# Four waits of TensorE in a graph network: sums of the first geglu quarter, a low part of step 0, last thirds of the last chunk, and the time of a load

## The chip, the cores and the metric

The kernel runs on one core of one Trainium2 chip. The time is device microseconds of one execution, the median of three runs. The profile is of one execution, with a span of its own.

## The reference

A graph network on 1024 nodes with 512 features, 16384 edges, and four transformer layers between two graph convolutions, all in fp32. Cut to what matters:

```python
h = gcn(batchnorm(relu(layernorm(x))), src, dst, gcn_in_w, gcn_in_b)
for i in range(4):
    q = ln(h) @ Wq[i]; k = cond @ Wk[i]; v = cond @ Wv[i]      # 16 groups of 64 nodes, 256 cond rows each
    h = h + softmax(q k^T / 8) v @ Wo[i]                        # 8 heads of 64
    val, gate = split(ln(h) @ geglu_w[i] + geglu_b[i])          # 2 x 2048 columns
    h = h + (val * gelu(gate)) @ ffo_w[i] + ffo_b[i]
out = x + gcn(h, src, dst, gcn_out_w, gcn_out_b) + relu(layernorm(x))
```

## The kernel before

TensorE (PE) does nearly all the work. Most products are not run as fp32 matmuls: an operand is split into a high part of twelve bits (names with h: `ah`, `bh`, `gr`, `gha`), a low part (l) and a third (s, made of the two), and three quick matmuls give what one slow one would. ACT makes high parts, DVE low parts by a SCALAR_TENSOR_TENSOR of two operands in SBUF, and POOL or DVE the thirds. `left_parts` does so for the moving side.

A layer goes through these stages:

- **Attention**, in steps g = 0 to 6 and one more. A step makes the scores of 128 nodes (`sc`, L831), their softmax (`nmax` and `pr` on DVE, the exponential on ACT), and beside them keys and values of the next step (`k`, `v`; `split_cond` splits the condition rows `ct` into `ah_c`, `al_c` and `as_c`, two tiles of each for a step; `base_of` makes one block of the final sum's base in two steps of a layer: the Relu `again` on ACT and two adds on DVE).
- **The first geglu quarter**, class `Quad`, four pieces c = 0 to 3. It runs as plain fp32 by a scheme of seven products, of which sums of sums are formed on DVE: `u2 = b + s1`, `u3 = c + u2`, `g1 = d + u3`, `g0 = c + u2`, with b, c and d the banks `gb`, `gc`, `gd`. Products 5, 6 and 4 fill b, c and d; product 3 then adds into c, so PE waits for u3 to have read it, and product 2 adds into d, so PE waits for g1. Between the sums `fill()` puts the next piece of splitting the right operands for the other quarters (`gr`, `gl`, lines 1017, 1025 and 1037) on DVE's queue. POOL sums thirds there (L1039) and weight sums (L1081).
- **The other three quarters**, chunks (r, c) with split operands (L1109). `split_rest` makes thirds of the next chunk's weights on POOL (`gsb`, `gs`). In the last chunk of a layer, (R-1, KC-1), `output.split(0, nc.gpsimd)` splits the first gated tile of the output product: `ah_f` on ACT, `al_f` on DVE, `as_f` on POOL.
- **The output product**, 16 units of 24 matmuls (L1252). Unit n fetches the gated tile `fr` of unit n + 2, splits that of n + 1, and runs what a table `beside` names for n. In the last layer that table loads the edge counts (`ce`, eight tiles, issued by POOL) for the last convolution, takes `w_out`, and splits it.

The order of each engine's instructions is fixed when the program is built: a scheduler orders what is not pinned, `pin` and `in_order` keep the written order, `tc.issue_after(x)` puts instructions behind x in the order, and `waiting_for(x, engine)` adds a real wait on x. Tiles come from pools: `slots` has 35 buffers of 512 KB, taken in turn, so a new tile waits for the last reader of the buffer that it gets. PSUM has 8 banks.

Of the kernel before, what the change touches and what calls it, by code (L numbers as in the profile page):

```python
# [15 lines left out]
OP = mybir.AluOpType  # L16
# [5 lines left out]
TINY = 2.0 ** -12  # L22
# [4 lines left out]
def gnn_kernel(  # L27
# [26 lines left out]
    nc = tc.nc  # L54
# [10 lines left out]
    KC = D // P  # L65
# [4 lines left out]
    R = DFF // D  # L70
# [235 lines left out]
    def twelve_bits(t):  # L306
        return t.bitcast(F32R)
# [3 lines left out]

    def left_parts(x, name, t=None):

        parts = [slots_of(len(x), f"{n}_{name}") for n in ("ah", "al", "as")]
        for h, l, s, x in zip(*parts, x):
            nc.scalar.mul(twelve_bits(h), x, INWARD * TINY)  # L318
            nc.vector.scalar_tensor_tensor(twelve_bits(l), h, -1.0 / TINY, x, OP.mult, OP.add)  # L319
            if t:  # L320
                t.tensor_tensor(twelve_bits(s), h, l, OP.subtract)  # L321
                continue
            for k in range(2):
                nc.gpsimd.tensor_tensor(twelve_bits(s)[:, k, :], h[:, k, :], l[:, k, :],  # L324
                                        OP.subtract)
        return parts
# [16 lines left out]
                        twelve_bits(s)[:, k, :], hk, -TINY, lk, OP.mult, OP.add)  # L343
        return parts

    def split_cond(l, g):
        if g < NG:
            if l == 0:
                save_cond(g)
            conds[g] = left_parts(raw_x.pop((l, g)), f"c_{l}_{g}")  # L350

    conds = {}

# [592 lines left out]
    class Quad:  # L946
# [27 lines left out]
        def rest(self, fill):  # L974
            n, bias = self.n, gcols[:, self.cv:self.cv + 1]
            b, c, d = (bank(f"{x}_{n}") for x in ("gb", "gc", "gd"))
            u2, u3 = (acc_tile(f"g{x}_{n}") for x in ("u2", "u3"))
            g0, g1 = (t512(f"{x}_{n}") for x in ("g0", "g1"))
            f0, f1 = self.f.of(self.c)

            def add(to, x, y):
                self.last = pin(nc.vector.tensor_tensor(to, x, y, OP.add))

            self.product(5, b, True, pin)
            add(u2, b, self.s1)
            fill()
            self.product(6, c, True, pin)
            add(u3, c, u2)
            fill()
            self.product(4, d, True, pin)  # L990
            add(g1, d, u3)
            self.gate(g1, n)
            fill()
            self.product(3, c, False, pin)
            add(g0, c, u2)
            self.gate(g0, n)
            fill()
            self.product(2, d, False, pin)
            add(d, d, u2)
            pin(nc.vector.scalar_tensor_tensor(f0, self.a, bias, g0, OP.add, OP.mult))  # L1000
            pin(nc.vector.scalar_tensor_tensor(f1, d, bias, g1, OP.add, OP.mult))
            self.f.store(self.c)
            fill()
            fill()
# [196 lines left out]
    class Output:  # L1201
# [8 lines left out]
                self.raw[n] = slot(f"fr_{self.l}_{n}")  # L1210
                nc.sync.dma_start(self.raw[n], f_dram[s, 2 * u:2 * u + 2].rearrange("c p n -> p c n"))

        def split(self, n, t=nc.vector):
            if n in self.raw:
                self.f[n] = left_parts([self.raw.pop(n)], f"f_{self.l}_{n}", t)

        def fetch_w(self, u):
            if u < UNITS:
# [206 lines left out]
    for l in range(L):  # L1425
# [157 lines left out]
        for g in range(NG - 1):  # L1583
            if g == NG - 2:
                take_ln3()
                raw = load_geglu(l, 0)
                add_bias(nc.vector)
            if not g:
                probs = scores(l, g, qT, kTs.pop(g))
            if g == NG - 2:  # L1590
                with waiting_for(scores.last, mybir.EngineType.Pool):
                    left = geglu_weights(l, 0, *raw)
            wo_flow = out_parts(l, wo) if not g else iter(())
            wo = next(wo_flow, wo)
            if g in (1, 2):
                fetch_x(2 * l + g - 1)
            k = keys(l, g + 1, wk, 1 if l == 0 and g == 0 else 0)
            for i, u in enumerate(k):
                u.begin()
                if not i:  # L1600
                    for end in ends:
                        end()
                if i > 1:
                    k[i - 2].end()
                next(wo_flow, None)
            k[-2].end()
            for _ in wo_flow:
                pass
            v = values(l, g + 1, wv)
            with in_order(mybir.EngineType.DVE) if g == NG - 2 else nullcontext():  # L1610
                oT = mix(l, g, probs, vs.pop(g), (
                    k[-1].end, nothing, lambda: (v[0].begin(), g == NG - 2 and
                                                 add_bias(nc.vector, *range(4)))))
            if g < NG - 2:
                probs = scores(l, g + 1, qT, kTs.pop(g + 1))
                with tc.issue_after(scores.last.ins):
                    oT = oT()
            if g == NG - 2:
                oT = oT()
                ln3_norm(g - 2, g - 1, behind=mix.last)  # L1620
                add_bias(nc.gpsimd, g - 2, g - 1)
            if g in (1, 2):
                with tc.issue_after(scores.last.ins):
                    base_of(2 * l + g - 1)
            if l == 0:
                fetch_cond(g + 3)
            split_cond(l, g + 2)
            if l:
                load_cond(l, g + 3)
            v[1].begin()  # L1630
            v[0].end()
            v[2].begin()
            v[1].end()
            pieces = attn_out(l, g, oT, wo, pin) if g < NG - 2 else iter(())
            next(pieces, None)
            if g in (3, 5):
                moments_into(mv_kept[:, 2 * (g - 3):2 * (g - 1)], [h[g - 3], h[g - 2]],
                             f"ln3_{l}_{g - 3}")
            if g == NG - 2:
                for nb in range(4):  # L1640
                    ln3_turn(nb, each=pin)
            v[3].begin()
            next(pieces, None)
            v[2].end()
            next(pieces, None)
            ends = [v[3].end]
            if g == NG - 3:
                scale_kept()
            if g == NG - 2:
                for nb in range(4, 6):  # L1650
                    ln3_turn(nb, each=pin)
                for nb in (g - 2, g - 1):
                    ln3_sums(nc.gpsimd, nb)
            if l == 0 and g + 3 < NG:
                turn_cond(g + 3, each=pin)
# [30 lines left out]
        def fill(n=1):  # L1686
            for _ in range(n):
                next(parts, None)
# [64 lines left out]
                load()  # L1753
        sum_chunk(2)

        def split_rest(short):
            long = begin_split(0, False)
            next(long, None)
            with waiting_for(split_left.low, mybir.EngineType.Pool):
                for flow in short, long:  # L1760
                    for _ in flow:
                        pass
# [4 lines left out]
        for r in range(1, R):  # L1767
            f = Gated(l, r)
            for c in range(KC):
                n = (r - R + 2) * KC + c  # L1770
                if n == -1:
                    output.fetch_w(0)
                if (r, c) == (R - 1, KC - 2):
                    output.fetch(0)
                chunk = ready.pop(0)
                flow = chunk.steps(lambda: before and sum_chunk(1))
                chunk.f = f
                next(flow)
                if 0 < n < 5:
                    next(ahead)  # L1780
                for _ in islice(short, 2):
                    pass
                next(flow)
                if before:
                    split_rest(short)
                    load()
                for _ in parts:
                    pass
                if (r, c) == (R - 1, KC - 1):
                    with in_order(mybir.EngineType.Activation), in_order(mybir.EngineType.DVE), \  # L1790
                            in_order(mybir.EngineType.Pool):
                        output.split(0, nc.gpsimd)
                    output.fetch(1)
                for step in range(3):
                    if before:
                        next(before, None)
                    next(flow)
                    if step == 1 and not before:
                        split_rest(iter(()))
                        load()  # L1800
                before = flow
                short = begin_split(0, True)
                if n == 0:
                    next(ahead)
# [9 lines left out]
        if last:  # L1814
# [15 lines left out]
                nonlocal w_out  # L1830
                w_out = right_parts(w_out, "w_out")

            beside = {8: begin_last, 9: fetch_counts, 12: fetch_last, 15: split_last}
        else:
            half = range(4), range(4, 8)
            wk, wv = [[], [], []], [[], [], []]
# [121 lines left out]
```

## Time and profile before

| | |
|---|---|
| median of 3 runs | 2298.52 us (2296.37 to 2298.68) |
| the profiled execution | 2296.64 us |
| its span | 2294.9 us |
| granted clock of PE | 1.0 throughout |
| busy: PE, DVE, ACT, POOL | 2265.4, 1734.6, 1168.7, 747.1 us |

A row of a timeline is: start, length, engine, line, operation, output <- inputs, shape, how many alike, and in brackets the idle time ahead of it and who ended it. A row of the waits is: who waited <- for whom, then us in total, how many times, and the longest. Lines are those of the kernel before.

### The profile page before, as it was taken

How to read it: one execution, taken by the hardware profiler on the slowest of the kernel's cores; microseconds unless marked ns; L12 is line 12 of the kernel's file. 1: busy time of each engine (PE TensorE's matmuls, PEld its weight loads, DVE VectorE, ACT ScalarE, POOL GpSimd, SP SyncE). 2: the span in 40 equal slices, each digit the busy share in tenths (PEclk: the TensorE clock that was granted, in tenths of full speed). 3: DMA queues.
4: the chain of work that ended last, by engine and by line, in shares of the span. 5: the costliest groups of instructions: out<-in, count | busy, mean ns of one | idle time of the engine just before them, and what ended most of it. 6: DMA issues, size and time to landing. Idle time of an engine off the chain costs nothing. (4 is left out here: it accounts for less than half of the span.)

```text
span 2294.9 us, 34482 instructions
## 1 busy us (share of the span) xinstructions
PE 2265.4 (99%) x12496; PEld 1754.5 (76%) x12496; DVE 1734.6 (76%) x3172; ACT 1168.7 (51%) x2245; POOL 747.1 (33%) x647
## 2 busy tenths in 40 slices
PE   8999999999999999999999999999999999999999
PEld 5678887587887888488887888578788888668777
DVE  9886556999986555989987554989987554899965
ACT  7555445565355445465356444556437444556521
POOL 1121213486021224377021222368112112268301
PEclk9999999999999999999999999999999999999999
DMA  6042211234411101133521111133531111043551
GB/s 206 2 152 70 74 61 42 83 120 152 169 46 65 61 29 42 60 119 99 200 92 65 51 38 42 42 107 100 184 138 56 37 52 51 1 129 111 184 173 57
DMA packets 144113, 204.42 MB, mean 89 GB/s; under 512 B 11240, under 2 KB 68912, under 8 KB 143936
## 3 DMA queue, kind: packets, MB, share of 16 engines
q1 hardware_dynamic: 141840, 196.72, 26.0%
q0 software_dynamic: 1376, 4.30, 0.6%
q8 instruction: 103, 1.69, 0.3%
q10 hardware_dynamic: 720, 1.11, 0.1%
q14 instruction: 74, 0.61, 0.1%
HBM read 151.75 MB, written 50.34 MB: 88 GB/s over the span
## 5 line engine op out<-in xcount | busy, mean ns | idle before, releaser
L324 POOL TENSOR_TENSOR as_c<-ah_c,al_c 128x512 fp32r<-128x512 f32 x128 | 197.7, 1574 | 901.0 <-DVE al_c L319 679.9
L1123 ACT ACTIVATE g<-g 128x512 f32<-128x512 f32 x192 | 112.5, 586 | 152.8 <-PE g L1109 151.5
L381 ACT ACTIVATE k<-k 128x512 f32<-128x512 f32 x125 | 73.0, 585 | 193.0 <-PE k L370 193.0
L1252 PE MATMUL fx<-bs_wff,as_f 128*128 128x512 f32 x512 | 159.0, 390 | 0.6 <-DVE as_f L321 0.6
L1252 PE MATMUL fy<-bl_wff,al_f 128*128 128x512 f32 x512 | 158.8, 390 | 0.6 <-DVE al_f L319 0.5
L318 ACT ACTIVATE ah_f<-fr 128x1024 fp32r<-128x1024 f32 x64 | 67.9, 1061 | 177.3 <-PE fy L1252 98.8
L1252 PE MATMUL fy<-bh_wff,ah_f 128*128 128x512 f32 x512 | 157.8, 390 | 0.2 <-ACT ah_f L318 0.2
L386 DVE COPY kT<-k 128x512 f32<-128x512 f32 x54 | 37.2, 689 | 156.8 <-PE k L370 156.8
L370 PE MATMUL v<-bh_wv,ah_c 128*128 128x512 f32 x508 | 140.9, 399 | 0.0
L370 PE MATMUL v<-bs_wv,as_c 128*128 128x512 f32 x508 | 137.1, 393 | 2.6 <-ACT v L381 2.6
L1050 POOL TENSOR_TENSOR gsa<-gha,gla 128x512 fp32r<-128x512 f32 x96 | 124.1, 1315 | 40.2 <-DVE gla L1045 40.2
L370 PE MATMUL v<-bl_wv,al_c 128*128 128x512 f32 x508 | 136.6, 390 | 0.0
L843 ACT ACTIVATE pr<-sc,nmax 128x256 f32<-128x256 f32 x256 | 118.1, 474 | 35.0 <-DVE nmax L838 34.5
L370 PE MATMUL k<-ah_c,bh_wk 128*128 128x512 f32 x500 | 135.1, 392 | 0.0
L381 ACT ACTIVATE v<-v 128x512 f32<-128x512 f32 x127 | 75.0, 591 | 116.9 <-PE v L370 116.9
L370 PE MATMUL k<-as_c,bs_wk 128*128 128x512 f32 x500 | 132.1, 395 | 1.8 <-ACT k L381 1.8
L370 PE MATMUL k<-al_c,bl_wk 128*128 128x512 f32 x500 | 133.8, 389 | 0.0
L1109 PE MATMUL g<-gr,gha 128*128 128x512 f32 x384 | 120.0, 394 | 0.0
L1109 PE MATMUL g<-gr,gsa 128*128 128x512 f32 x384 | 119.9, 393 | 0.0
L1109 PE MATMUL g<-gl,gla 128*128 128x512 f32 x384 | 118.3, 389 | 0.0
L370 PEld LDWEIGHTS v<-bs_wv,as_c 128*128 128x128 f32 x508 | 93.2, 188 | 27.7 <-ACT v L381 5.7
L370 PEld LDWEIGHTS v<-bh_wv,ah_c 128*128 128x128 f32 x508 | 92.6, 188 | 27.9 <-issue 9.2
(321 smaller groups left out, 5814.3 us busy)
## 6 DMA issues: line engine op xcount, KB each, us to landing
f_dram<-fT SPq DMA_DIRECT2D x128, 256.0 KB, 2.1
fr<-f_dram SPq DMA_DIRECT2D x64, 512.0 KB, 4.1
ct<-cond_dram SPq DMA_DIRECT2D x48, 512.0 KB, 4.7
wff<-in_L_gnn_ffo_w_dram SPq DMA_DIRECT2D x32, 512.0 KB, 5.2
gxb<-in_L_gnn_geglu_w_dram SPq DMA_DIRECT2D x96, 128.0 KB, 2.5
gxa<-in_L_gnn_geglu_w_dram SPq DMA_DIRECT2D x96, 128.0 KB, 2.6
cond<-in_L_gnn_cond_dram SPq DMA_DIRECT2D x32, 256.0 KB, 4.2
cond_dram<-ct SPq DMA_DIRECT2D x16, 512.0 KB, 3.3
```

Of the source, the lines that this page charges most:

```text
L318: nc.scalar.mul(twelve_bits(h), x, INWARD * TINY)
L324: nc.gpsimd.tensor_tensor(twelve_bits(s)[:, k, :], h[:, k, :], l[:, k, :], OP.subtract)
L370: pin(nc.tensor.matmul(self.bank, twelve_bits(left[k // 2])[:, k % 2, self.c * P:(self.c + 1) * P], twelve_bits(right[k // 2])[:, k % 2, : ...
L381: nc.scalar.mul(self.bank, self.bank, 1.0 + TINY)
L386: nc.vector.tensor_copy(self.to(), self.bank)
L843: nc.scalar.activation(pr3[:, a, :], ps3[:, a, :], AF.Exp, bias=nmax[:, a:a + 1], accum_out=tot[:, a:a + 1])
L1050: split_left.last = pin(t.tensor_tensor(s_at, h_at, l_at, OP.subtract))
L1109: pin(nc.tensor.matmul(to, self.part(i, which)[:, k, :], self.rights[i][which].bitcast(F32R)[:, k, :], start=start and k == 0, stop=stop a ...
L1123: pin(nc.scalar.mul(to, to, 1.0 + TINY))
L1252: pin(nc.tensor.matmul(to, twelve_bits(left[which][0])[:, k, b * P:(b + 1) * P], twelve_bits(right[which])[:, k, :], start=u == 0 and whic ...
```

## The change

It has four parts.

- **A.** In `Quad.rest` the number of fills between the sums changes: in c=0 one more fill behind u2, in c=1 and c=2 u3 directly behind u2 and both fills behind u3.
- **B.** `split_cond` splits its two tiles one by one. In step 0 of each layer the second is put behind `scores.last`, the last instruction of the softmax. `base_of` now also waits for that instruction on ACT.
- **C.** In the last chunk `split_rest` is called from within `output.split`, between al_f and as_f, and its POOL instructions wait for al_f instead of for the low part of the chunk's weights.
- **D.** In the last layer the counts are loaded at unit 11 instead of 9.

```diff
@@ left_parts
-    def left_parts(x, name, t=None):
+    def left_parts(x, name, t=None, between=None):
...
-            nc.vector.scalar_tensor_tensor(twelve_bits(l), h, -1.0 / TINY, x, OP.mult, OP.add)
+            left_parts.low = nc.vector.scalar_tensor_tensor(twelve_bits(l), h, -1.0 / TINY, x,
+                                                            OP.mult, OP.add)
+            if between:
+                between()
@@ split_cond
-    def split_cond(l, g):
+    def split_cond(l, g, behind=None):
...
-            conds[g] = left_parts(raw_x.pop((l, g)), f"c_{l}_{g}")
+            conds[g] = [[], [], []]
+            for i, x in enumerate(raw_x.pop((l, g))):
+                with tc.issue_after(behind.ins) if behind and i else nullcontext():
+                    for to, of in zip(conds[g], left_parts([x], f"c_{l}_{g}_{i}")):
+                        to.extend(of)
@@ Quad.rest
             add(u2, b, self.s1)
-            fill()
+            at_once = self.c in (1, 2)
+            if not at_once:
+                fill()
+            if not self.c:
+                fill()
             self.product(6, c, True, pin)
             add(u3, c, u2)
+            if at_once:
+                fill()
             fill()
             self.product(4, d, True, pin)
             add(g1, d, u3)
@@ Output.split
-        def split(self, n, t=nc.vector):
+        def split(self, n, t=nc.vector, between=None):
             if n in self.raw:
-                self.f[n] = left_parts([self.raw.pop(n)], f"f_{self.l}_{n}", t)
+                self.f[n] = left_parts([self.raw.pop(n)], f"f_{self.l}_{n}", t, between)
@@ the steps of attention
             if g in (1, 2):
-                with tc.issue_after(scores.last.ins):
+                with tc.issue_after(scores.last.ins), \
+                        waiting_for(scores.last, mybir.EngineType.Activation):
                     base_of(2 * l + g - 1)
...
-            split_cond(l, g + 2)
+            split_cond(l, g + 2, None if g else scores.last)
@@ split_rest and the chunks
-        def split_rest(short):
+        def split_rest(short, behind=None):
...
-            with waiting_for(split_left.low, mybir.EngineType.Pool):
+            with waiting_for(behind or split_left.low, mybir.EngineType.Pool):
...
+                the_last = (r, c) == (R - 1, KC - 1)
                 if before:
-                    split_rest(short)
+                    if not the_last:
+                        split_rest(short)
                     load()
...
-                if (r, c) == (R - 1, KC - 1):
+                if the_last:
...
-                        output.split(0, nc.gpsimd)
+                        output.split(0, nc.gpsimd, lambda: split_rest(short, left_parts.low))
@@ the table of the last layer
-            beside = {8: begin_last, 9: fetch_counts, 12: fetch_last, 15: split_last}
+            beside = {8: begin_last, 11: fetch_counts, 12: fetch_last, 15: split_last}
```

The order of PE's and of POOL's instructions is the same before and behind the change. That of DVE, ACT and SP is not.

Part A on DVE, piece c=1 of the first quarter of layer 0; `gu2`, `gu3`, `g1` and `g0` are the sums u2, u3, g1 and g0, and `gl` and `gr` the fills. Before:

```order
L982 TENSOR_TENSOR gu2_0_0_1_18372<-gb_0_0_1_18369,gs1_0_0_0_18128 128x512
L1037 SCALAR_TENSOR_TENSOR gl_0_6_18354<-ln3T_0_1_0_17699,gr_0_6_18352 128x512
L982 TENSOR_TENSOR gu3_0_0_1_18373<-gc_0_0_1_18370,gu2_0_0_1_18372 128x512
L1017 SCALAR_TENSOR_TENSOR gr_0_5_18383<-ln3S_0_1_17702,gt_0_5_0_18385 128x512
L982 TENSOR_TENSOR g1_0_0_1_18375<-gd_0_0_1_18371,gu3_0_0_1_18373 128x512
L1017 SCALAR_TENSOR_TENSOR gr_0_5_18383<-ln3S_0_1_17702,gt_0_5_1_18391 128x512
L982 TENSOR_TENSOR g0_0_0_1_18374<-gc_0_0_1_18370,gu2_0_0_1_18372 128x512
```

The same place behind the change (L989 is the old L982, L1030 the old L1017):

```order
L989 TENSOR_TENSOR gu2_0_0_1_18379<-gb_0_0_1_18376,gs1_0_0_0_18128 128x512
L989 TENSOR_TENSOR gu3_0_0_1_18380<-gc_0_0_1_18377,gu2_0_0_1_18379 128x512
L1030 SCALAR_TENSOR_TENSOR gr_0_5_18365<-ln3S_0_1_17702,gt_0_5_0_18367 128x512
L1030 SCALAR_TENSOR_TENSOR gr_0_5_18365<-ln3S_0_1_17702,gt_0_5_1_18391 128x512
L989 TENSOR_TENSOR g1_0_0_1_18382<-gd_0_0_1_18378,gu3_0_0_1_18380 128x512
L1038 SCALAR_TENSOR_TENSOR gl_0_5_18394<-ln3S_0_1_17702,gr_0_5_18364 128x512
L989 TENSOR_TENSOR g0_0_0_1_18381<-gc_0_0_1_18377,gu2_0_0_1_18379 128x512
```

The fill between u2 and u3 is gone (it stands ahead of u2 now), and two fills, not one, stand between u3 and g1.

Part B on DVE, step 0 of layer 1; `al_c_1_2_1` is the second low part, `ol` and `os` are parts of the attention's output of the step. Before:

```order
L319 SCALAR_TENSOR_TENSOR al_c_1_2_0_21145<-ah_c_1_2_0_21143,ct_1_2_0_20865 128x1024
L319 SCALAR_TENSOR_TENSOR al_c_1_2_1_21146<-ah_c_1_2_1_21144,ct_1_2_1_20866 128x1024
L838 TENSOR_REDUCE nmax_1_1_0_21101<-sc_1_1_0_21081 128x2
L838 TENSOR_REDUCE nmax_1_1_1_21111<-sc_1_1_1_21082 128x2
L846 RECIPROCAL inv_1_1_0_21107<-tot_1_1_0_21104 128x2
```

And behind the change, the end of the same softmax:

```order
L853 RECIPROCAL inv_1_1_3_21137<-tot_1_1_3_21134 128x2
L855 TENSOR_SCALAR pr_1_1_3_21133<-pr_1_1_3_21133,inv_1_1_3_21137 128x256 x2
L899 SCALAR_TENSOR_TENSOR ol_1_0_21078<-oh_1_0_21077,po_1_0_21001 128x512
L319 SCALAR_TENSOR_TENSOR al_c_1_2_1_0_21151<-ah_c_1_2_1_0_21150,ct_1_2_1_20866 128x1024
L900 TENSOR_TENSOR os_1_0_21079<-oh_1_0_21077,ol_1_0_21078 128x512
```

The second al_c moved from ahead of the four maxima to behind the last normalisation and ol. On ACT the Relu `again_2` stood ahead of the first v scaling of step 0 and now stands in step 1, between the copy of v and the third scaling.

## The prediction

> **What bounds the kernel now.** I read three views, in this order. The page's first part says whether one engine carries the span. The waits, grouped by who waited for whom and taken on PE alone, say what could be won at all. The timelines of the four stretches that the change touches then give the sizes.
>
> ```profile
> PE 2265.4 (99%) x12496; PEld 1754.5 (76%) x12496; DVE 1734.6 (76%) x3172; ACT 1168.7 (51%) x2245; POOL 747.1 (33%) x647
> ```
> ```profile
> engine line waited for: us in total, times, longest us
> PE gc L301 <- DVE gu L982: 4.4, 8, 0.7
> ...
> PE v L370 <- ACT v L381: 2.6, 5, 1.0
> ...
> PE g L1109 <- DVE g L1127: 1.2, 4, 0.3
> ...
> PE fx L1252 <- DVE as_f L321: 0.6, 1, 0.6
> PE fy L1252 <- DVE al_f L319: 0.5, 1, 0.5
> ...
> PE fy L1252 <- ACT ah_f L318: 0.2, 1, 0.2
> ```
>
> PE is busy for all but 29.5 us (2294.9 minus 2265.4), so nothing but PE's idle time can be won, and the change adds no matmul and takes none away. The six rows are the waits that its four parts aim at: the first geglu quarter (gc, eight times, twice a layer), step 0 of attention (v; four of the five are the step 0s of the four layers), the last geglu chunk (g, once a layer), and unit 11 of the last layer's output product (three rows). They hold 4.4 + 2.6 + 1.2 + 1.3 = 9.5 us of idle time.
>
> What such a wait costs is a little more than its idle time. PE in the first quarter of layer 0:
>
> ```profile
> 423.16 1.88 PE L301 MATMUL gd<-ln3S,ges 128*128 128x512 f32 x4
> 425.48 1.98 PE L301 MATMUL gc<-ln3S,wgate 128*128 128x512 f32 x4 [0.43 <-DVE gu L982]
> 427.30 1.88 PE L301 MATMUL gd<-ln3T,ges 128*128 128x512 f32 x4
> 429.01 1.88 PE L301 MATMUL gb<-ln3S,ges 128*128 128x512 f32 x4
> ...
> 432.45 1.88 PE L301 MATMUL gd<-ln3S,ges 128*128 128x512 f32 x4
> 435.00 1.98 PE L301 MATMUL gc<-ln3S,wgate 128*128 128x512 f32 x4 [0.67 <-DVE gu L982]
> ```
>
> A product starts 1.71 to 1.72 us after the one ahead of it (427.30 to 429.01). Around the first wait it is 2.32 (0.60 late), and 1.82 to the next (0.10 more). So a wait of 0.43 costs 0.70, its idle time plus 0.27; the second is 2.55 - 1.72 = 0.83, plus 0.10: 0.93. I price the rest in this way, as idle time plus 0.27 for each wait.
>
> **A, the first quarter's sums.** What can go: 0.70 + 0.93 = 1.63 a layer, 6.5 in four. DVE and POOL beside the rows above:
>
> ```profile
> 423.05 0.69 DVE L982 TENSOR_TENSOR gu<-gb,gs 128x512 f32<-128x512 f32 x1
> 423.65 1.17 DVE L1037 SCALAR_TENSOR_TENSOR gl<-ln3T,gr 128x512 fp32r<-128x512 f32 x1
> 424.74 0.68 DVE L982 TENSOR_TENSOR gu<-gc,gu 128x512 f32<-128x512 f32 x1
> 425.34 1.15 DVE L1017 SCALAR_TENSOR_TENSOR gr<-ln3S,gt 128x512 fp32r<-128x512 f32 x1
> ...
> 427.02 1.16 DVE L1017 SCALAR_TENSOR_TENSOR gr<-ln3S,gt 128x512 fp32r<-128x512 f32 x1
> ...
> 431.21 0.80 DVE L1025 SCALAR_TENSOR_TENSOR gl<-ln3S,gr 128x512 fp32r<-128x512 f32 x1
> 431.93 1.21 DVE L1017 SCALAR_TENSOR_TENSOR gr<-ln3S,gt 128x512 fp32r<-128x512 f32 x1
> 433.06 0.68 DVE L982 TENSOR_TENSOR gu<-gb,gs 128x512 f32<-128x512 f32 x1
> ```
> ```profile
> 422.68 4.95 POOL L1039 TENSOR_TENSOR gr<-gl,gt 128x512 fp32r<-128x512 f32 x3 [1.74 <-DVE gl L1037]
> ```
>
> DVE runs without a gap here, so each row starts where the queue lets it. The second sum u3 (424.74) stands behind the fill of 423.65, and PE's third product behind u3. An unhindered row takes a slot of 0.60 (433.06 after 431.93 + 1.13; 424.74 + 0.60 = 425.34). The fills that read only SBUF are stretched to a slot of 1.07 to 1.13 while POOL sums; the sums, which read PSUM, are not.
>
> At c=1 the change lets u3 follow u2: u3 starts at 423.65 and ends at 424.33, before PE wants it (423.16 + 1.72 = 424.88), so the wait of 0.70 goes. But now two fills stand between u3 and the next sum g1, and PE's last product, which adds into d, cannot start before g1 has read d. It would want to start at 424.88 + 1.72 = 426.60. From 424.25 the two fills take 1.20 (neither stretched), 1.85 (0.72 + 1.13, what the pair at 431.21 took) or 2.15 (1.07 + 1.08, what the two at 425.34 and 427.02 took); with 0.68 for g1 and 0.06 to PE it starts at 426.19, 426.84 or 427.14, which is 0, 0.24 or 0.54 late. I take 0.54, since POOL has three sums of gr queued in just these microseconds. With the 0.10 behind it that is 0.64 in place of 0.70: the wait moves from the third product to the last.
>
> At c=2 DVE is free for the first fill at 431.21 as before, since the rows ahead of it wait for PE. Two fills, then u2 and u3: u3 starts 1.85 + 0.60 after 431.21, at 433.66, and ends at 434.34; with 0.06 PE starts at 434.40 instead of 434.17 (432.45 + 1.72), 0.23 late where it was 0.83 (0 with unstretched fills, 0.53 with both at their worst). Then two fills ahead of g1 again: 434.26 + 1.20 to 1.85, so PE's last product is 0 to 0.6 late. POOL's sums thin out there; I take 0.10 late. So 0.23 + 0.10 + 0.10 = 0.43 in place of 0.93.
>
> A layer goes from 1.63 to 1.07, and A gains 0.56 x 4 = 2.2. The ends: 6.5 if no fill is stretched; with all three pairs at 2.15, 0.64 + 0.63 + 1.03 = 2.30 a layer, a loss of 2.7. The fill that moves into c=0 lies in DVE's waits for PE there.
>
> **B, step 0 of attention.** The scores' matmuls, the softmax on DVE and ACT, and the product that waits, in layer 1 at step 0 and then at step 1:
>
> ```profile
> 717.31 1.96 PE L831 MATMUL sc<-kT,qT 64*64 64x256 f32 x32
> ...
> 724.50 1.21 PE L370 MATMUL v<-bs_wv,as_c 128*128 128x512 f32 x4 [0.47 <-ACT v L381]
> ```
> ```profile
> 717.04 2.11 DVE L319 SCALAR_TENSOR_TENSOR al_c<-ah_c,ct 128x1024 fp32r<-128x1024 f32 x1 [1.64 <-ACT ah_c L318]
> 719.07 1.28 DVE L838 TENSOR_REDUCE nmax<-sc 128x2 f32<-128x512 f32 x2
> ```
> ```profile
> 723.85 0.59 ACT L381 ACTIVATE v<-v 128x512 f32<-128x512 f32 x1
> ```
> ```profile
> 748.57 1.96 PE L831 MATMUL sc<-kT,qT 64*64 64x256 f32 x32
> ...
> 755.14 1.09 PE L370 MATMUL v<-bs_wv,as_c 128*128 128x512 f32 x4
> ```
> ```profile
> 749.70 1.29 DVE L838 TENSOR_REDUCE nmax<-sc 128x2 f32<-128x512 f32 x2 [1.46 <-PE sc L831]
> ```
> ```profile
> 754.37 0.59 ACT L381 ACTIVATE v<-v 128x512 f32<-128x512 f32 x1
> ```
>
> At step 0 the first maximum starts 1.76 after the scores (719.07 - 717.31), held by the second al_c, and ACT's scaling of v ends at +7.13. At step 1 they stand at +1.13 and +6.39, and PE takes v at +6.57 without a wait. The change moves that al_c behind the whole softmax and the base's Relu off ACT's queue ahead of it, so step 0 becomes like step 1: 0.18 are to spare. Gain: idle 1.0 in layer 0 and 0.47 in three others, 2.4, plus 4 x 0.27: 3.5. I take 3.4; the low end is 2.4, if 0.25 stays in each layer. What the moved pieces could hold up: al_c (1.2 to 2.1) now stands ahead of os, which PE does not take for some microseconds, and its third part on POOL is needed only by the keys of the step after; the Relu, now a step later, stands behind one v scale and ahead of another whose product PE takes late in the step. The order on SP changes only by loads that are wanted a step later. I cost all this at nothing.
>
> **C, the last chunk.**
>
> ```profile
> 2141.59 1.90 DVE L319 SCALAR_TENSOR_TENSOR al_f<-ah_f,fr 128x1024 fp32r<-128x1024 f32 x1 [0.62 <-ACT ah_f L318]
> 2143.41 0.74 DVE L1175 SCALAR_TENSOR_TENSOR fT<-g,gcols,g 128x512 f32<-128x512 f32 x1
> ...
> 2151.51 1.23 DVE L319 SCALAR_TENSOR_TENSOR al_f<-ah_f,fr 128x1024 fp32r<-128x1024 f32 x1
> ```
> ```profile
> 2141.11 1.30 POOL L1050 TENSOR_TENSOR gsb<-ghb,glb 128x512 fp32r<-128x512 f32 x1 [2.35 <-DVE gs L1045]
> ```
> ```profile
> 2142.43 1.30 ACT L1136 ACTIVATE g<-g,gcols 128x512 f32<-128x512 f32 x2
> ```
>
> POOL's gsb starts before al_f and al_f takes 1.90 instead of 1.23. Behind the change gsb waits for al_f, which ends at 2142.82; the next row on DVE then waits for the first of ACT's two (2142.43 + 0.65 = 2143.08) and starts some 0.3 earlier than at 2143.41, and so does all behind it, down to the sum that PE waits for by 0.3. Gain between 4 x 0.2 and the whole of it, 1.2 + 4 x 0.27 = 2.3; I take 1.5 (0.3 a layer, and a bit of what follows a wait). POOL's gsb starts 1.7 later; the products with gsb and gs are the chunk's last, and as_f is wanted only by the output product behind them.
>
> Beside gsb, al_f is held for most of gsb's instruction: gsb ends at 2142.41, and 2142.41 + 1.23 is 2143.64, close to al_f's end at 2143.49. Two fills in a row took 0.80 and 1.21 beside POOL in part A, where an unhindered row of their shape takes 0.68. The Trainium skill, SBUF — State Buffer, section "SBUF: two separate sides", says that a DVE operation with two SBUF inputs and a GpSimd operation that reads SBUF exclude each other for a whole instruction, whichever starts first. By that rule both fills of a pair are held wherever POOL has work waiting, which speaks against part A: its sum would be the worst end, a loss of 2.7. The trace agrees in al_f and at c=1, and less at 431.21, where only the second of the pair is held.
>
> **D, the counts.** At unit 9 the eight count tiles take slots of the pool ahead of the parts of unit 11, and ACT's ah_f of unit 11 gets a slot that unit 10 frees only with its last use.
>
> ```profile
> 2209.40 1.06 ACT L318 ACTIVATE ah_f<-fr 128x1024 fp32r<-128x1024 f32 x1 [9.82 <-PE fy L1252]
> ```
> ```profile
> fr<-f_dram SPq DMA_DIRECT2D x64, 512.0 KB, 4.1
> ```
>
> ACT idled 9.82 us for that. Taken at unit 11, the counts leave unit 11 a slot freed some 10 us earlier, and ah_f, al_f and as_f (1.06, 1.23 and 1.23) are done well before PE wants them. The three waits go: 1.3 + 3 x 0.27 = 2.1. What moves later is eight loads issued by POOL, some 5 us, and they are first read two units and more behind their landing. The least D can give is nothing, if another load then comes late. I take 2.1.
>
> **The sum** is 2.2 + 3.4 + 1.5 + 2.1 = 9.2 us off the profiled execution's 2296.64 (1.7 around the span of 2294.9 included), 2287.4. That execution lies 1.9 below the median of the runs, 2298.52, and inside their spread; from the median the same step gives 2289.3.
>
> **The rivals.** *All of the quarter's waits go* (0.12): the fills are not stretched in their new places. For it speaks that POOL's first sums may be done earlier; against it, that DVE has no gap there. 9.2 - 2.2 + 6.5 = 13.5: 2285.0. *The quarter loses* (0.18): every pair is held by POOL. For it speak the three stretched fills of c=1, against it the pair of 2.01 at 431.21. 9.2 - 2.2 - 2.7 = 4.3: 2294.2. *The counts get in the way of the fr loads* (0.13): D gives nothing, or up to 2 us late loads besides. For it speaks the median of 4.1 us for 512 KB, against it that these loads are issued a unit and more ahead. 2291.4 to 2293.4. *Slower* (0.07): the counts, taken later, hold the slots that the fr tiles of units 14 and 15 need, and those loads are issued only when the unit ahead of them ends. Then load and ah_f stand bare on PE's path, 4.1 + 1.06 = 5.2 us a unit at least and twice that if the transfers crowd: 10.4 for two, against the 7.1 of A, B and C. It decides as soon as two units are hit, and gives 2301.8 at the least.
>
> **How the numbers follow.** The forecast as worked out has 0.50. About 0.2%, 4.6 us, is what a measurement of this kernel can tell from no change. Faster by more than that are the forecast, the first rival, nearly all of the third and a good part of the second: 0.82. Within it lies the rest of the second and third, 0.11; slower is 0.07. The range goes from just under the first rival, 2284.8, to 2296.0, beyond the second with a little of what the runs scatter (2.3 us between the three).
>
> **What would show it.** Right: the row of PE's waits for gu at L982's new place falls from 8 waits to few, and waits of the last product for g1 appear; nmax starts 1.13 behind the scores in every step and the v row shrinks to 0.2; the al_f of the last chunk takes 1.2; the three rows of unit 11 are gone. Wrong: fills of 0.68 throughout the quarter (first rival), late products of 0.9 at c=2 (second), fr landings later than ah_f's turn in units 12 to 15 (third and fourth), or new waits of PE at the keys of step 1.

## The result and the profile after

| | before | after |
|---|---|---|
| median of 6 runs | 2297.27 us (2296.16 to 2298.68) | 2288.95 us (2287.43 to 2290.26) |
| the profiled execution | 2296.64 us | 2290.13 us |
| its span | 2294.9 us | 2288.4 us |

The ratio is 0.9963, with a 95% interval from 0.9954 to 0.9973: 8.3 us less, where 9.2 were forecast. The predicted time was 2289.3.

The span of the profiled execution fell by only 6.5 us. The timeline of PE tells why; its first product of layer 0 (q) starts, before and then after, at

```profile
136.50 1.16 PE L370 MATMUL q<-bh_ln,ah_wq 128*128 128x512 f32 x4
```
```profile
139.02 1.17 PE L377 MATMUL q<-bh_ln,ah_wq 128*128 128x512 f32 x4
```

The first convolution, which the change does not touch, took 2.5 us longer in this execution. Of that, 1.7 lie at one place: eight matmuls of `begun_k` took 5.37 us instead of 3.67, and between 85 and 90 us the granted clock of PE was 0.66 in this execution and 1.00 in that of before. In the eight executions profiled below the convolution ends between 136.3 and 138.2. I therefore compare stages on PE: attention from the first `sc` of a layer to the first `gb`, the quarter from there to the first `g`, the chunks from there to the first `fy`, and the last output product from there to the first product of the last convolution (layers 0 to 3, us):

| stage | before | after | change | forecast |
|---|---|---|---|---|
| attention (B) | 247.92, 241.22, 241.19, 241.17 | 246.57, 240.35, 240.37, 240.37 | -3.84 | -3.4 |
| first quarter (A) | 35.81, 35.81, 35.81, 35.82 | 35.23, 35.17, 35.72, 35.17 | -1.96 | -2.2 |
| chunks (C) | 116.54, 116.54, 116.51, 116.50 | 116.29, 116.29, 116.25, 116.33 | -0.93 | -1.5 |
| last output product (D) | 89.89 | 87.62 | -2.27 | -2.1 |

The four together are 9.0 us in these two executions, 8.3 in the medians. The page's first part and PE's waits after:

```profile
PE 2264.2 (99%) x12496; PEld 1755.7 (77%) x12496; DVE 1729.5 (76%) x3172; ACT 1169.8 (51%) x2245; POOL 737.4 (32%) x647
```
```profile
PE gd L301 <- DVE g L989: 2.2, 4, 0.6
...
PE gc L301 <- DVE gu L989: 0.6, 1, 0.6
...
PE v L377 <- ACT v L388: 0.3, 1, 0.3
```

PE is busy for as long as before, to 1.2 us. Eight waits for u3 have become one, and four new ones for g1 have come (gd <- g). Of the five v rows one is left, and the rows of the last chunk and of unit 11 are gone. Now the places one by one. A, the timelines of PE, DVE and POOL in layer 0, c=1 and c=2:

```profile
426.04 1.88 PE L301 MATMUL gc<-ln3S,wgate 128*128 128x512 f32 x4
428.47 1.98 PE L301 MATMUL gd<-ln3T,ges 128*128 128x512 f32 x4 [0.55 <-DVE g L989]
...
433.72 1.88 PE L301 MATMUL gd<-ln3S,ges 128*128 128x512 f32 x4
435.74 1.98 PE L301 MATMUL gc<-ln3S,wgate 128*128 128x512 f32 x4
437.56 1.96 PE L301 MATMUL gd<-ln3T,ges 128*128 128x512 f32 x4
```
```profile
424.21 0.68 DVE L989 TENSOR_TENSOR gu<-gb,gs 128x512 f32<-128x512 f32 x1
425.00 0.69 DVE L989 TENSOR_TENSOR gu<-gc,gu 128x512 f32<-128x512 f32 x1
425.61 2.20 DVE L1030 SCALAR_TENSOR_TENSOR gr<-ln3S,gt 128x512 fp32r<-128x512 f32 x2
427.74 0.68 DVE L989 TENSOR_TENSOR g<-gd,gu 128x512 f32<-128x512 f32 x1
...
432.42 1.87 DVE L1030 SCALAR_TENSOR_TENSOR gr<-ln3S,gt 128x512 fp32r<-128x512 f32 x2
```
```profile
423.86 2.80 POOL L1052 TENSOR_TENSOR gr<-gl,gt 128x512 fp32r<-128x512 f32 x2 [1.51 <-DVE gl L1050]
```

The third product (426.04) waits no more; the last (428.47) is 0.71 late, behind two fills that took 2.20 while POOL summed. At c=2 the third product is 0.30 late (435.74 - 433.72 - 1.72), and there is 0.10 behind it.

B, step 0 of layer 1, on PE, DVE and ACT:

```profile
717.67 1.96 PE L838 MATMUL sc<-kT,qT 64*64 64x256 f32 x32
...
724.23 1.08 PE L377 MATMUL v<-bs_wv,as_c 128*128 128x512 f32 x4
```
```profile
718.80 1.29 DVE L845 TENSOR_REDUCE nmax<-sc 128x2 f32<-128x512 f32 x2 [3.04 <-PE sc L838]
...
725.00 1.22 DVE L319 SCALAR_TENSOR_TENSOR al_c<-ah_c,ct 128x1024 fp32r<-128x1024 f32 x1
```
```profile
723.46 0.59 ACT L388 ACTIVATE v<-v 128x512 f32<-128x512 f32 x1
```

The first maximum starts 1.13 behind the scores, ACT's scaling ends at +6.38, PE takes v at +6.56 without a wait: step 1's numbers of before (1.13, 6.39, 6.57). al_c stands at 725.00, behind all of it.

C, the last chunk of layer 3, on DVE, POOL and ACT:

```profile
2137.59 1.23 DVE L319 SCALAR_TENSOR_TENSOR al_f<-ah_f,fr 128x1024 fp32r<-128x1024 f32 x1 [0.63 <-ACT ah_f L318]
2139.15 0.75 DVE L1188 SCALAR_TENSOR_TENSOR fT<-g,gcols,g 128x512 f32<-128x512 f32 x1 [0.34 <-ACT g L1149]
```
```profile
2138.96 1.30 POOL L1063 TENSOR_TENSOR gsb<-ghb,glb 128x512 fp32r<-128x512 f32 x1 [4.20 <-DVE al_f L319]
```
```profile
2138.44 1.29 ACT L1149 ACTIVATE g<-g,gcols 128x512 f32<-128x512 f32 x2
```

al_f takes 1.23, not 1.90, and POOL follows it. But the next row of DVE now waits 0.34 for ACT, which it did not before. PE at the same place, from gsb to the first product of the next stage, before and after:

```profile
2147.56 0.61 PE L1109 MATMUL g<-gr,gsb 128*128 128x512 f32 x2
2148.46 0.73 PE L1109 MATMUL g<-gr,gsb 128*128 128x512 f32 x2 [0.28 <-DVE g L1127]
...
2149.68 0.61 PE L1252 MATMUL fy<-bh_wff,ah_f 128*128 128x512 f32 x2
```
```profile
2143.11 0.61 PE L1122 MATMUL g<-gl,gs 128*128 128x512 f32 x2
2143.56 1.37 PE L1122 MATMUL g<-gr,gsb 128*128 128x512 f32 x4
...
2145.44 0.62 PE L1265 MATMUL fy<-bh_wff,ah_f 128*128 128x512 f32 x2
```

It took 2.12 (2147.56 to 2149.68) and takes 1.88. Three pairs of matmuls at the 0.45 of an unhindered pair (2143.11 to 2143.56) would be 1.36, so a lateness of 0.76 has shrunk to 0.52 and not gone, though the waits have no row for it any more.

D, units 12 to 15 of the last output product. The fr loads from 2190 to 2225, with their times to landing, the last ah_f on ACT, its third part on DVE, and the start of unit 15 on PE:

```profile
L1224 SPq DMA_DIRECT2D fr<-f_dram x5: 359/360/467, 2194.3 to 2212.0; - x5
...
DMA to landing us min/median/max: 3.5/4.9/11.2
```
```profile
2223.28 1.06 ACT L318 ACTIVATE ah_f<-fr 128x1024 fp32r<-128x1024 f32 x1 [6.14 <-DMA fr<-f_dram]
```
```profile
2225.70 1.23 DVE L324 TENSOR_TENSOR as_f<-ah_f,al_f 128x1024 fp32r<-128x1024 f32 x1
```
```profile
2227.61 0.62 PE L1265 MATMUL fy<-bh_wff,ah_f 128*128 128x512 f32 x2
```

PE has no wait left there. But the load of unit 15, issued at 2212.01 behind two loads of `w_out` and beside the last of the counts, took 11.2 us, and its third part is done at 2226.93, 0.7 us before that unit starts.

### The profile page after: what moved, and what is told of

It is laid out like the page before. It is cut to its first block, busy times and chain, and to the rows that moved or that the text cites. A ratio compares the mean times of both kernels' runs of the same rounds, so it can differ in the third digit from the quotient of the medians.

```text
span 2288.4 us, 34506 instructions
## 1 busy us (share of the span) xinstructions
PE 2264.2 (99%) x12496; PEld 1755.7 (77%) x12496; DVE 1729.5 (76%) x3172; ACT 1169.8 (51%) x2245; POOL 737.4 (32%) x647
## 5 line engine op out<-in xcount | busy, mean ns | idle before, releaser
L845 DVE TENSOR_REDUCE nmax<-sc 128x2 f32<-128x512 f32 x128 | 83.0, 678 | 44.0 <-PE sc L838 44.0
```

The source lines that it names most:

```text
L845: nc.vector.tensor_reduce(nmax, ps3, AX.X, OP.max, negate=True)
```

## The experiments

The first four kernels each carry one part of the change alone, on one chip with 31 runs of the kernel before (median 2296.71).

**Part A alone.** The edit is the part of the diff under `Quad.rest`, nothing else.

> Part A alone on the kernel before (the fills of the first quarter, nothing else). My theory: the wait moves from product 3 to product 2. The quarter, from PE's first gb to its first g, shrinks from 35.81 us a layer to between 35.1 and 35.8, PE waits four times for g1 (0.5 to 0.6 each), and attention (247.9 and 3 x 241.2), the chunks (116.5) and the last output product (89.9) keep their lengths to 0.1. About 2 us faster in all. Rival, that the parts need each other (the quarter starts at another phase of POOL's work when attention is shorter): the quarter alone gains nothing or all of 1.7 a layer.

Measured: 2295.64 us, ratio 0.9994 (0.9985 to 1.0004). The quarter is 35.18, 35.72, 35.17 and 35.17, the other stages stand as before, 2.0 us less in all. PE's waits:

```profile
PE gd L301 <- DVE g L982: 2.2, 4, 0.5
...
PE gc L301 <- DVE gu L982: 0.6, 1, 0.6
```

So A does by itself what it does in the whole: four waits for g1 in place of four for u3, and in one layer the wait at c=2 stays long (that layer gains 0.1 and not 0.6). With the whole change it was layer 2, here layer 1, with the same instructions.

**Part B's al_c alone.**

```diff
-            split_cond(l, g + 2)
+            split_cond(l, g + 2, None if g else scores.last)
```

with the new `split_cond`; the base stays where it was.

> The first half of part B alone: the second al_c of step 0 behind the softmax, while the base's Relu stays ahead of it on ACT. My theory: al_c is what held the first maximum, so attention shrinks by 0.8 us in layers 1 to 3 and by most of 1.3 in layer 0, 3 to 3.8 in all, nearly as with both halves. Rival: ACT's Relu (0.84) stands on the path too, and without its move half of the gain or more is missing (1 to 2 us).

Measured: 2293.10 us, ratio 0.9986 (0.9976 to 0.9995). Attention takes 246.35, 240.35, 240.31 and 240.36, as with the whole change (246.57, 240.35, 240.37, 240.37). The second low part was all that held step 0; the other half of B, the base behind the softmax, brings nothing that can be seen beside the 0.2 by which layer 0 differs from run to run.

**Part C alone.** The edits under `left_parts`, `Output.split` and `split_rest`.

> Part C alone: POOL's last thirds of the last chunk wait for al_f. My theory: al_f takes 1.2 instead of 1.9, and the chunks of a layer shrink from 116.5 by 0.2 to 0.3, 1.0 in all; all other stages as before. Rival: the chunk's end is bound by ACT's two gelus, and nothing is gained.

Measured: 2295.50 us, ratio 0.9997 (0.9988 to 1.0007). The chunks take 116.29, 116.30, 116.28 and 116.28: 0.94 less, 0.23 a layer, as in the whole.

**Part D alone.** 9 becomes 11 in the table of the last layer.

> Part D alone: the counts at unit 11. My theory (slots): the three waits of unit 11 go and the last output product shrinks from 89.89 to 87.6, nothing else moves. Rival (transfers): the fr loads of units 12 to 15 come late beside the counts and part of the 2.2 is given back, so 88 to 89.

Measured: 2294.64 us, ratio 0.9992 (0.9982 to 1.0002). The last output product takes 87.60, 2.29 less. The medians of the four runs lie 1.1, 3.6, 1.2 and 2.1 below that of before, 8.0 together, beside 8.3 for the whole change: within the scatter the parts add up. Singly, only the interval of al_c leaves out 1; the stages are what shows the others.

**The second fill elsewhere.** The changed kernel, with one fill between u3 and g1 at c=1 and c=2, one behind g1, and two more at c=3.

```diff
             add(u3, c, u2)
-            if at_once:
-                fill()
             fill()
             self.product(4, d, True, pin)
             add(g1, d, u3)
+            if at_once:
+                fill()
...
-            fill()
+            if not at_once:
+                fill()
...
-                first_chunk.extend([[parts], [long] * 3, [short], [short] * 4, [], []])
+                first_chunk.extend([[parts], [long] * 3, [parts, short], [short] * 4, [], []])
```

> The changed kernel with one fill fewer between u3 and g1 in c=1 and c=2 (one instead of two) and one fewer at their ends; the four fills go behind g1 (one each in c=1 and c=2) and into c=3 (one behind u2, one behind g1). My theory (PE's wait for g1 is the pair of fills held by POOL ahead of it): the four waits for g1 (0.55 each) and the waits for u3 at c=2 are gone, the quarter shrinks from 35.17 to 35.72 us to 34.4 to 34.7, about 3 to 5 us in all. Rival (DVE is simply full in this stage): the waits move on to product 3 or 2 of c=2 or c=3 and the quarter stays at 35 or above.

Measured: 2287.80 us, ratio to before 0.9961 (0.9947 to 0.9975). The quarter falls to 34.24, 34.70, 34.72 and 34.72, and the waits for g1 are gone; three waits for u3 of up to 0.3 are left. The chunks rise to 117.21 to 117.28, which neither the theory nor the rival had. PE's waits, PE and ACT at the first chunk of layer 0:

```profile
PE g L1123 <- ACT g L1137: 3.3, 4, 0.8
...
PE gc L301 <- DVE gu L989: 0.9, 3, 0.3
```
```profile
446.81 0.70 PE L1123 MATMUL g<-gr,gsa 128*128 128x512 f32 x2 [0.83 <-ACT g L1137]
```
```profile
445.46 0.72 ACT L979 ACTIVATE g<-g,gcols 128x512 f32<-128x512 f32 x1 [2.98 <-DVE g L989]
446.09 1.06 ACT L1137 ACTIVATE g<-g 128x512 f32<-128x512 f32 x2
```

The fills that were moved to c=3 make the quarter's last sums late, ACT's gelu with them, and the first chunk waits up to 0.8 us in each layer. Over four layers the quarter takes 138.4 where the profiled execution of the changed kernel took 141.3, 2.9 won, and the chunks 469.0 in place of 465.2, 3.8 given back. Against the run with the counts at 10, whose quarters take 142.8 with the changed kernel's instructions, 4.4 are won. The ratios to before, 0.9961 here and 0.9963 for the changed kernel, show no difference. The queue of DVE has no free place for these fills at the quarter's end.

**POOL kept away from the fills.** The changed kernel with its fills where they were, but POOL's two gr sums of that piece behind g1 at c=1:

```diff
             add(g1, d, u3)
+            if self.c == 1:
+                with waiting_for(self.last, mybir.EngineType.Pool):
+                    while later:
+                        later.pop(0)()
...
-            pin(nc.gpsimd.tensor_tensor(s.bitcast(F32R)[:, k, :], low[:, k, :], less[k],
-                                        OP.subtract))
+            def third(k=k):
+                pin(nc.gpsimd.tensor_tensor(s.bitcast(F32R)[:, k, :], low[:, k, :], less[k],
+                                            OP.subtract))
+            if name.endswith("6"):
+                later.append(third)
+            else:
+                third()
```

> The changed kernel with POOL's two sums of gr_6 (and what is queued behind them on POOL) waiting for g1 of c=1; DVE's order is that of the changed kernel. My theory (POOL holds the two fills): the pair ahead of g1 at c=1 takes 1.28 instead of 2.20, PE's wait for g1 at c=1 (0.55) goes, and later fills, which POOL's sums now meet, are stretched instead, so c=2 may wait more. Rival (two fills in a row cost DVE that much by themselves): the pair still takes 2.2 and the wait stays.

Measured: 2286.17 us, ratio 0.9954 (0.9938 to 0.9970). The quarter takes 34.90, 34.91, 34.89 and 34.90, the chunks 116.3. DVE, POOL and PE, c=1 and c=2 of layer 0:

```profile
423.16 1.28 DVE L1034 SCALAR_TENSOR_TENSOR gr<-ln3S,gt 128x512 fp32r<-128x512 f32 x2
...
432.28 1.81 DVE L1042 SCALAR_TENSOR_TENSOR gl<-ln3S,gr 128x512 fp32r<-128x512 f32 x2
```
```profile
425.19 3.27 POOL L1059 TENSOR_TENSOR gr<-gl,gt 128x512 fp32r<-128x512 f32 x2 [5.29 <-DVE g L989]
```
```profile
425.31 1.88 PE L301 MATMUL gd<-ln3T,ges 128*128 128x512 f32 x4
...
434.75 1.98 PE L301 MATMUL gd<-ln3T,ges 128*128 128x512 f32 x4 [0.35 <-DVE g L989]
```

The same pair of fills takes 1.28 where it took 2.20, and the last product of c=1 (425.31) starts without a wait. Nothing else about the pair was changed, so it is POOL that stretches the fills; the wait at c=1 is shown to be POOL's doing. At c=2 POOL's weight sums still stretch a pair to 1.81, and the wait for g1 has moved there. The Trainium skill, SBUF — State Buffer, section "SBUF: two separate sides", says that a DVE operation with two SBUF inputs and a GpSimd operation that reads SBUF exclude each other, and that the one that starts first goes through. The pair of 2.20 beside POOL, 0.92 more than without it, agrees.

**The counts at unit 10.** The changed kernel with 10 in place of 11.

> The changed kernel with the counts at unit 10 instead of 11. Theory of the slots: taking eight tiles shifts which buffer the parts of the unit two further on get, so the three waits come back at unit 12 and the last output product is 89 to 90 us instead of 87.6. Rival (it was the transfers' time, not the slots, that mattered between 9 and 11): something between 87.6 and 88.8, with late fr loads to be seen.

Measured: 2289.37 us, ratio 0.9968 (0.9955 to 0.9980). The last output product takes 88.61, 1.0 more than at 11 and 1.3 less than at 9, inside the rival's range and not the theory's. DMA issues between 2195 and 2225, ACT and PE:

```profile
fr<-f_dram SPq DMA_DIRECT2D x3, 512.0 KB, 8.6
```
```profile
2213.98 1.06 ACT L318 ACTIVATE ah_f<-fr 128x1024 fp32r<-128x1024 f32 x1 [8.20 <-DMA fr<-f_dram]
```
```profile
2217.61 0.73 PE L1265 MATMUL fx<-bs_wff,as_f 128*128 128x512 f32 x2 [0.53 <-DVE as_f L324]
```

No wait of PE stands at unit 12, where the theory of the slots put it. The wait is at unit 13. Its load was issued at 2204.71, behind seven of the counts' eight; the changed kernel issued it at 2199.75, ahead of them all. It then took 9.2 us (8.6 is the median of the three in this stretch, 4.1 that of the whole kernel before), ah_f waited for it, and as_f came late. That a slot held the issue is likely, since ah_f of unit 12, which waited for PE, starts within 0.01 us of it; the trace does not name what SyncE waited for. So late issue and slow transfer add up here. Of the three places tried, at 9 ah_f of unit 11 lacks a slot, at 10 the load of unit 13 is late, at 11 neither is.

This run shows something else. Up to the counts its program is that of the changed kernel, yet its quarter takes 35.61, 35.72, 35.72 and 35.72. The pair of fills ahead of u2 at c=2 took 2.25 in layer 0 here and 1.87 in the profiled execution of the changed kernel. So the quarter has two lengths, 35.2 and 35.7, and the stretch of this pair is what differs. The changed kernel's own execution has both lengths. The first fill of that pair and POOL's weight sum beside it, in layer 1 (35.17) and then in layer 2 (35.72):

```profile
959.48 0.68 DVE L1030 SCALAR_TENSOR_TENSOR gr<-ln3S,gt 128x512 fp32r<-128x512 f32 x1
```
```profile
959.66 1.09 POOL L1094 TENSOR_TENSOR gxa<-gxa 128x256 f32<-128x256 f32 x1
```
```profile
1486.48 1.24 DVE L1030 SCALAR_TENSOR_TENSOR gr<-ln3S,gt 128x512 fp32r<-128x512 f32 x1
```
```profile
1486.44 0.73 POOL L1094 TENSOR_TENSOR gxa<-gxa 128x256 f32<-128x256 f32 x1
```

In layer 1 the fill starts first and POOL's sum is the long one; in layer 2 POOL's sum starts 0.04 ahead and the fill is the long one. The twelve quarters of the three kernels with these fills (the whole change, part A alone, this run) all divide so. In the short ones, 35.17 to 35.23, the fill takes 0.68 to 0.73 and the sum 1.06 to 1.29; in the long ones, 35.61 to 35.72, the fill takes 1.12 to 1.24 and the sum 0.72 to 0.73. In two of the short ones the sum starts 0.02 to 0.03 ahead and is still the one held, but the profile's times on POOL are rough. So a few hundredths of a microsecond between two queues decide the length; no run moved POOL's weight sums alone to try it. Over the four layers part A is worth 2.0 us in the profiled execution of the change and 0.5 in this one (143.25 to 142.77).

**Both remedies, the best version.** The kernel with POOL's sums behind g1, and at c=2 alone one fill ahead of g1 and one behind it:

```diff
-            if at_once:
+            if self.c == 1:
                 fill()
...
             add(g1, d, u3)
...
+            if self.c == 2:
+                fill()
```

> The changed kernel with two edits: at c=1 GpSimd's two gr_6 sums wait for the last product's own sum (as in the run before), and at c=2 one fill instead of two stands between the third product's sum and the last one's, the second following behind the last one's; c=1 keeps its two fills ahead. Theory (what is left of the wait at c=2 is the fill pair of 1.81 us ahead of the last sum): the idle of 0.35 us at c=2 and its 0.27 us behind go, the quarter comes down from 34.90 to about 34.3 us in each layer (20 products of 1.716), the chunks stay at 116.3, and the span of the run before, 2284 to 2286 us, becomes about 2283.5; the fall against the kernel before is about 13 us, ratio 0.9945. Rival (VectorE's work only moves into c=3 and lets the gelu of the first chunk start later, as in the run with spread fills): the quarter comes down as well, but a wait of 0.5 to 0.8 us stands ahead of the chunks' first product, chunks 117.0 to 117.3, and the time stays at about 2286, ratio 0.9955.

Measured: 2283.76 us (2283.36 to 2285.05, 5 runs), against 2296.34 for the kernel before on the same chip, ratio 0.9942 (0.9928 to 0.9955). The quarter takes 34.38, 34.38, 34.39 and 34.39, the chunks 116.27 to 116.35. PE and DVE of layer 0:

```profile
429.57 1.81 DVE L1036 SCALAR_TENSOR_TENSOR gr<-ln3S,gt 128x512 fp32r<-128x512 f32 x2
```
```profile
430.86 1.88 PE L301 MATMUL gd<-ln3S,ges 128*128 128x512 f32 x4
432.83 1.98 PE L301 MATMUL gc<-ln3S,wgate 128*128 128x512 f32 x4
434.65 1.88 PE L301 MATMUL gd<-ln3T,ges 128*128 128x512 f32 x4
```

Both waits for g1 are gone, and the one fill moved behind g1 at c=2, not out to c=3, keeps the chunks where they were; the rival fell. What is left at c=2 is 0.25 at the third product and 0.10 behind it, from the pair of 1.81 ahead of u2. Its median lies 5.2 below that of the changed kernel, which was not run beside it. The quarters account for 3.8 of that (141.3 to 137.5 over four layers); the rest is not assigned, though the changed kernel's quarters can be longer than in its profiled execution, as the run with the counts at 10 shows.

## Why the prediction was right

**A came out at its size, by two errors that cancel and by luck.** The wait moved from the third product to the last as worked out, and POOL was the reason. At c=1 it was dearer: 0.71 + 0.10 late instead of 0.54 + 0.10. The pair took about the 2.15 reckoned as its worst (2.13 from its start to g1's). The step that failed was the start of the pair. I let u3 follow u2 after 0.60; it followed after 0.79 (424.21 to 425.00), so all behind it came 0.19 later. In all four layers, at c=1, 2 and 3, it is 0.78 or 0.79; u3 reads what u2 writes, which is the likely reason. At c=2 it was 0.30 + 0.10, and 0.08 more one product on, against 0.43. Against the dearer c=1 stands a gain that I had not seen, since it is no row in the waits. From start to start, PE's third product of c=3 was 0.11 late before, with 0.10 behind it, and neither is there after. In layer 0 the sum of what is late went from 1.84 to 1.29, the stage from 35.81 to 35.23. One layer got only 0.1, and in the run with the counts at 10 every layer got only 0.1 to 0.2, by the stretched pair at c=2. That three of four layers were short in the execution profiled was luck that the sum did not contain. The rivals "all of the quarter's waits go" and "the quarter loses" both fell: every pair at c=1 was held, but not every pair at c=2. That both fills of a pair are held wherever POOL has work waiting was too strong: at c=2 the first fill took 0.68 to 0.73 in three layers, and POOL's sum was held instead.

**B's step came out at its size, and the stage gained 0.4 more.** Idle time plus 0.27 gave 0.74 in layers 1 to 3 and 1.27 in layer 0. Step 0, from its scores to the next, went from 31.26 to 30.50 us in layer 1 and from 33.53 to 32.31 in layer 0, in the four layers 3.44 less, and became like step 1. So the mechanism stands. The stage as a whole gained 0.80 to 0.87, and 1.35; the 0.1 a layer beyond step 0 lies in hundredths in the later steps, and I cannot place it. That the Relu costs nothing where it went was right; the run without it shows that it cost nothing where it was, either.

**C was over-sized: 0.93 for 1.5.** The step that failed is the bit added "of what follows a wait". The step ahead of it said that the row behind al_f would then wait for ACT and start some 0.3 earlier. It does: DVE waits 0.34 for ACT, and against PE's gsb (2147.56 before, 2143.56 after) the row starts 0.26 earlier (2143.41 and 2139.15). PE got 0.24 of it (2.12 to 1.88). Its lateness became shorter and did not go: it gave back no more than it shrank by, and what follows a wait is still paid. So a layer gained 0.23 (0.93 in four) where 0.38 (1.5 in four) was taken.

**D was right: 2.27 for 2.1.** The three waits went. The cover that I named for the counts, loads "issued a unit and more ahead", is thinner than that sounds: at 11.2 us the last load left 0.7 us. The eight loads of the counts, put at some 5 us, landed 5.9 to 13.7 us after their issue, which cost nothing because they are first read some 11 us after the last has landed. The rival of crowded fr loads does happen one unit earlier, at 10, where late issue and crowding cost 1.0 us. The slower rival, loads held by slots until the unit ahead ends, did not come about: PE waited for no fr behind unit 11.

## What to carry to other kernels

When a queue without gaps holds a wait, moving an instruction in it moves the wait; price the new place with the stretched durations, and ask which engine does the stretching. Here it paid to hold back the idle partner (POOL, 32% busy): the four quarters went from 141.3 to 139.6 us. A fill moved by one place then took them to 137.5, where fills moved to the end of the stage gave back in the next stage about what they had brought. Read a stage from start to start on the bounding engine: two latenesses of 0.1 us were no row of the waits view and made a tenth of the first quarter's loss.

## What the runs showed of the hardware

- Two fills of 128x512 in fp32 on DVE took 1.28 us with POOL still, and 1.81, 1.87, 2.20 and 2.25 beside POOL's sums.
- The same instructions took 35.2 or 35.7 us in a quarter, from layer to layer and from run to run. In twelve quarters of three kernels, either the first fill of a pair was long (1.12 to 1.24) and POOL's sum beside it short (0.72 to 0.73), or the fill short (0.68 to 0.73) and the sum long (1.06 to 1.29).
- u3, which reads what the row ahead of it wrote, started 0.78 to 0.79 us behind it on DVE; unstretched rows of its size that do not started 0.60 behind.
- A load of 512 KB, 4.1 us from issue to landing in the median, took up to 11.2 us with five loads of the same size issued by POOL still in flight and two of its own queue just ahead of it.
